# Loads of x three stages later, and two stores a stage later, in a hand-ordered two-layer convolution kernel

## The chip, the cores and the metric

The kernel runs on one core of one Trainium2 chip. The metric is device time in microseconds (us) of one launch; the times shown are those of whole runs, and the profile is of one further execution, taken by the hardware profiler.

## The reference

The input is x, 32 images of 256 channels of 32 x 32 pixels in float32. Two layers follow each other, each added to its own input.

```python
def _gn(v, G=32, eps=1e-5):                # group norm: 32 groups of 8 channels, over all pixels
    ...
    return ((g - m) / jnp.sqrt(s + eps)).reshape(v.shape)

# layer 0: 3x3 convolution, 256 -> 256, with operands and result rounded to a short float format
x = x + _L0_conv_ref(_gn(x), L0_conv_weight, L0_conv_bias)
# layer 1: involution. Each pixel makes its own 7x7 weights, 16 groups of 16 channels
x = x + _L1_conv_ref(_gn(x), L1_conv_w1, ...)
#   y   = relu(bn(w1 @ x))                  256 -> 64 channels
#   w   = w2 @ y + b2                       64 -> 16 groups x 49 taps, for each pixel
#   out = sum over the 49 taps of w[group, tap, pixel] * x[channel, pixel + tap]
```

## The kernel before, in words

An image stays in SBUF as one tile `x_{b}` (128 partitions, 2 halves of the channels, 1024 pixels). The pool `xpool` has five such tiles, so the load of image b can start only when the last store of image b-5 has landed. The same tile is read by the first group norm, gets the convolution added to it, then the involution, and is stored.

The involution is done by TensorE as matrix products over a banded matrix. The path of these bands is what the DMA engines mostly carry:

- `weights(b, r0)` (line 402): TensorE makes the tap weights of four rows (line 410, into PSUM tiles `pw`), VectorE adds the bias and puts them into a ring in SBUF, `w_sb` (line 428).
- `scatter(b, k)` (line 466): seven DMAs of 160 KB, all on SyncE's queue, write the weights of eight rows from `w_sb` to a scratch tensor `wd` in DRAM (line 477). There are four such k for an image.
- `load_bands(b, k)` (line 479): sixteen DMAs of 70.2 KB read `wd` back into one of three `band` buffers (line 490). Fourteen of them are issued by GpSimd, two by SyncE (`SHARE = 8`).
- `sums(b, m)` (line 501): TensorE multiplies a band with the pixels (line 515); the band k serves m = 2k and 2k+1. `add_windows(b, m)` (line 523) lets VectorE add the result to x (line 531).

`front(b)` (line 284) is a generator that does everything of an image ahead of that: the sums and squares of the first group norm (ScalarE, line 219), the normalised image `xq` (line 278), 72 matmuls of the convolution (line 332), VectorE's rounding `q` and addition to x (lines 346, 348), the second group norm, the normalised `xn` (line 278), the 64 matmuls of `py` (line 380), the activation `y` (line 387), and the transposed pixels (lines 395, 399). Its first two steps are ScalarE's sums over the two halves of the freshly loaded x.

The order on every engine is written out by hand. The loop at the end goes over stages n; an image takes 16 stages, and each kind of work has a lag against its image. Work that is due in one stage is issued in the order of the loop's body, and each engine's queue holds it in that order. Several fronts are under way at once, of images up to three ahead, and in each stage the older image's front is issued first. Stages below are counted as n modulo 16, where stage 0 is `sums(b, 0)`:

| stage | on SyncE's queue before the change |
|---|---|
| 1 | load of x for image b+4 (`LOAD = -63`) |
| 3 | scatter k=0 of the next image, then two DMAs of band k=3 |
| 7 | scatter k=1 of the next image, then two DMAs of band k=0 of the next image |
| 8, 9 | (not SyncE: ScalarE's first sums over the x of image b+4, `FRONT = -56`) |
| 11 | scatter k=2 of the next image, two DMAs of its band k=1 |
| 12 | store of the first half of image b |
| 13 | scatter k=3 of the next image |
| 15 | store of the second half of image b, two DMAs of band k=2 of the next image |

`load_x` (line 102) issues two DMAs of 512 KB; `store` (line 533) one of 512 KB. The DMAs of SyncE use eight completion semaphores in turn, and so do those of GpSimd, so a DMA is issued only when the one eight places ahead of it has landed.

Of the kernel before, what the change touches and what calls it, by code (L numbers as in the profile page):

```python
# [14 lines left out]
B, C, H, W = 32, 256, 32, 32  # L15
# [28 lines left out]
M = K * SIDES  # L44
# [19 lines left out]
NPIX = 6  # L64
RING = 24
FRONT = -56
LOAD = -63
LEAD = 18


# [1 line left out]
def tile_quant_conv_then_involution(  # L72
# [29 lines left out]
    def load_x(b):  # L102
        xt = xpool.tile([P, CH, N], F32, tag="x", name=f"x_{b}")
        for h in range(CH):
            nc.sync.dma_start(xt[:, h], x[b, h * P : (h + 1) * P])
        return xt
# [15 lines left out]
    x_tiles = {0: load_x(0)}  # L122
# [75 lines left out]
    def quantize_weights():  # L198

        for kh in range(CH):  # L200
            nc.vector.tensor_scalar(wq[:, kh], staged[kh], F16_MAX, -F16_MAX, ALU.min, ALU.max)
            nc.gpsimd.memset(bands[kh], 0.0)
        nc.gpsimd.memset(w_sb, 0.0)
# [198 lines left out]
    def weights(b, r0):  # L402

        pws = [ps_w.tile([P, 2, 2, SW], F32, tag=f"pw{i}", name=f"pw{i}") for i in range(2)]
        for r in range(2):
            for t in range(T):
                for i in range(2):
                    half = slice(i * CR, (i + 1) * CR)
                    dj = slice(2 * t, min(2 * t + 2, K1))
                    nc.tensor.matmul(  # L410
                        pws[i][t * TW : (t + 1) * TW, r, : dj.stop - dj.start],
                        y_sb[b % 2][half, (r0 // 2 + r) * W : (r0 // 2 + r + 1) * W],
                        w2_sb[half, dj],
                        start=True,
                        stop=True,
                    )
        for i in range(2):
            for e in range(2):
                p = P if e == 0 else (K1 // 2) * TW
                for r, rows, d0, d1, at in ring_pieces(b, r0 + 2 * i):  # L420

                    to = w_sb[:p, e]
                    to = bass.AP(
                        tensor=to.tensor,
                        offset=to.offset + at * WB + K1 - 1 - d0,
                        ap=[to.ap[0], [WB, rows], [WB - 1, d1 - d0], [WIN, G]],
                    )
                    nc.vector.tensor_tensor(  # L428
                        to,
                        pws[i][:p, r : r + rows, e, d0 * G : d1 * G].rearrange("p r (d g) -> p r d g", g=G),  # L430
                        b2_sb[:p, e, d0 * G : d1 * G]
                        .unsqueeze(1)
                        .to_broadcast([p, rows, (d1 - d0) * G])
                        .rearrange("p r (d g) -> p r d g", g=G),
                        ALU.add,
                    )
# [29 lines left out]
    def scatter(b, k):  # L466

        at = (b * H + k * TR) % RING
        for dj in range(K1):
            t, e = divmod(dj, 2)  # L470
            to = bass.AP(
                tensor=wd.tensor,
                offset=wd.offset + k * TR * ROW + dj * WPIX + (K1 - 1 - dj) * WB,
                ap=[[WPIX, TW], [ROW, TR], [1, WB]],
            )
            rows = w_sb[t * TW : (t + 1) * TW, e, at : at + TR]
            nc.sync.dma_start(to, rows.rearrange("p s g r -> p s (g r)"))  # L477

    def load_bands(b, k):

        band = bands[(b * K + k) % NBAND]
        for i in range(JC):
            j = i // 2 + i % 2 * JC // 2
            src = bass.AP(
                tensor=wd.tensor,
                offset=wd.offset + k * TR * ROW + (j + PAD1) * WPIX,
                ap=[[ROW - 1, TR], [JC * WPIX, SIDES], [1, WPIX]],
            )
            queue = nc.sync if i % SHARE == SHARE - 1 else nc.gpsimd
            queue.dma_start(band[j::JC, :, j * WB : j * WB + WPIX], src)  # L490
# [10 lines left out]
    def sums(b, m):  # L501

        k, d = divmod(m, SIDES)
        j0 = 0 if d else PAD1
        band = bands[(b * K + k) % NBAND][:, d]
        px = pixels[(b * K + k) % NPIX][:, d]
        for h in range(CH):
            for v in range(2):
                for g, at, top, f, l in windows(b, m):
                    p = slice(g * KP, (g + 1) * KP)  # L510
                    of = band[p, g * XR + j0 * WB : g * XR + (j0 + WINI) * WB]
                    of = of.rearrange("p (j g r) -> p j g r", g=G, r=WIN)
                    for t in range(T):
                        a = h * T + t
                        nc.tensor.matmul(  # L515
                            at[t * TW : (t + 1) * TW, h, :, f - top : l - top],
                            px[p, a, v * GC : v * GC + TW],
                            of[:, :, 2 * a + v, f - top : l - top],
                            start=(h, v) == (0, 0),
                            stop=(h, v) == (CH - 1, 1),  # L520
                        )

    def add_windows(b, m):

        d = m % SIDES
        to = x_tiles[b].rearrange("p h (r c) -> p h r c", c=W)
        j0 = d * (JC - PAD1)
        for g, at, top, f, l in windows(b, m):
            x_at = to[:, :, f:l, j0 : j0 + WINI]
            of = at.rearrange("p h j r -> p h r j")[:, :, f - top : l - top]  # L530
            nc.vector.tensor_tensor(x_at, of, x_at, ALU.add)  # L531

    def store(b, k):

        cols = slice(k * NT, (k + 1) * NT)
        nc.sync.dma_start(out[b].rearrange("(h p) n -> p h n", p=P)[:, :, cols], x_tiles[b][:, :, cols])
# [3 lines left out]
    per = 2 * M  # L540

    def due(n, lag):

        b, i = divmod(n - lag, per)
        return (b, i) if 0 <= b < B else (None, None)

    with tc.manual_schedule():
        fronts = {}
        for n in range(FRONT, B * per + 2):
            b, i = due(n, FRONT)  # L550
            if i == 0:
                fronts[b] = front(b)
            later = list(fronts)
            for part in range(2):
                for b in list(later):
                    got = next(fronts[b], fronts)
                    if got is fronts:
                        fronts.pop(b)
                    if got is not LATER:
                        later.remove(b)  # L560
            if n == FRONT + CH:
                quantize_weights()
            b, i = due(n, 0)
            if b is not None and i % 2 == 0:
                sums(b, i // 2)
            b, i = due(n, 1)
            if b is not None and i % 2 == 0:
                add_windows(b, i // 2)
                if i // 2 == M - 1:
                    store(b, 1)  # L570
                    x_tiles.pop(b)

            b, i = due(n, 2)
            if b is not None and i == 2 * (M - 1 - SIDES):
                store(b, 0)
            b, i = due(n, -LEAD)
            if b is not None and i % 2 == 0:
                weights(b, i // 2 * WR)

            b, i = due(n, -LEAD + 1)  # L580
            if b is not None and i % 2 == 0:
                for k in range(K):
                    if i // 2 == min((k + 1) * TR // WR, H // WR - 1):
                        scatter(b, k)
            b, i = due(n, LOAD)
            if i == 0 and b > 0:
                x_tiles[b] = load_x(b)

            b, i = due(n, 3 - 4 * NBAND)
            if b is not None and i % 4 == 0:  # L590
                load_bands(b, i // 4)
# [37 lines left out]
```

## Time and profile before

| | |
|---|---|
| time, median of 3 runs | 1401.32 us (1395.67 to 1407.39) |
| the profiled execution's own time | 1399.26 us |
| its span, first to last instruction | 1397.5 us |
| TensorE matmul busy | 1263.0 us, 90% |
| GpSimd busy (DMA descriptors, nearly all) | 1009.8 us, 72% |
| VectorE busy | 926.6 us, 66% |
| ScalarE busy | 727.9 us, 52% |
| bytes moved by DMA | 369.33 MB, mean 264 GB/s |
| mean granted TensorE clock | 0.979 of full speed |

The busy times are sums over one engine's instructions; the issue of a DMA by SyncE is not counted as busy, and is seen in SyncE's own list of waits and in its timeline. The first matmul comes 18 us after the start, the first `add_windows` at 95.6 us, and from there an image takes 41.0 us on average, 2.56 us for a stage. The three loads of x for images 1 to 3 are issued at 21.3, 22.6 and 23.6 us.

### The profile page before, as it was taken

To read this page: it belongs to the slowest core of one execution; us is meant where nothing else is said; L and a number is where in the kernel's file an instruction comes from. 1 tells how busy PE (TensorE), PEld (TensorE's weight loads), DVE (VectorE), ACT (ScalarE), POOL (GpSimd) and SP (SyncE) were. 2 spreads that over 40 slices of the span, in tenths; PEclk is the share of its full clock that TensorE was granted. 3 is DMA by queue.
4 is the path that set the end of the run, shared out by engine and by line. 5 is a ranking of instruction groups with operands and counts; after the bars stand their busy time and mean duration, and the time that the engine had idled before them with its cause. 6 is when DMAs were issued, how large, how long until landed. Compare 5 with 4: busy or idle time off the path is not lost.

```text
span 1397.5 us, 70073 instructions
## 1 busy us (share of the span) xinstructions
PE 1263.0 (90%) x29440; PEld 801.1 (57%) x29440; DVE 926.6 (66%) x3179; ACT 727.9 (52%) x1699; POOL 1009.8 (72%) x1818
## 2 busy tenths in 40 slices
PE   4899999999999999998998999999999999999765
PEld 2455565556656566565655565655555655556544
DVE  3567677666776667676776666776666776777552
ACT  5865556455655546565554556463556564553200
POOL 9067777777777777778777777767776767777785
PEclk9999999999999999999999999999999999999876
DMA  6099999999999999999999999999999999999996
GB/s 215 16 248 276 253 283 289 280 274 272 286 284 274 287 278 281 278 285 274 280 287 272 272 273 282 263 278 275 273 282 267 265 282 277 282 264 269 252 257 187
DMA packets 366232, 369.33 MB, mean 264 GB/s; under 512 B 78624, under 2 KB 308192, under 8 KB 365664
## 3 DMA queue, kind: packets, MB, share of 16 engines
q1 hardware_dynamic: 279904, 235.72, 57.3%
q0 software_dynamic: 86016, 129.14, 34.7%
q8 instruction: 234, 3.83, 1.2%
q14 instruction: 78, 0.64, 0.2%
HBM read 183.81 MB, written 180.74 MB: 261 GB/s over the span
## 4 chain that ended last, share of the span: by engine, by line
PE 49%; DMA 30%; issue 6%; POOL 5%; DVE 4%; SPq 3%; ACT 2%; POOLq 0%; DVEq 0%; ACTq 0%
DMA band<-wd 23%; PE pc L332 20%; PE acc L515 15%; PE pw L410 9%; DMA wd<-w_sb 6%; POOL band L490 5%; PE py L380 3%; SPq L477 3%; DVE w_sb L428 2%; PE pt L395 2%; ACT junk L219 1%; DVE x L531 1%; DMA band<-in_w 1%; DMA x<-in_x 0%; ACT xn L278 0%
## 5 line engine op out<-in xcount | busy, mean ns | idle before, releaser
L490 POOL DMA_DIRECT2D band<-wd x1792 | 977.9, 548 | 375.4 <-DMA band<-wd 239.4
L428 DVE TENSOR_TENSOR w_sb<-pw,b_sb 128x16 f32<-128x16 f32 (+9 forms) x1920 | 454.3, 349 | 374.7 <-PE pw L410 362.0
L332 PE MATMUL pc<-xq,wq 128*128 128x496 f16 (+3 forms) x2304 | 535.1, 378 | 28.1 <-ACT xq L278 21.3
L515 PE MATMUL acc<-band,pixels 64*32 64x190 f32 (+1 forms) x16384 | 419.1, 323 | 73.8 <-DMA band<-wd 32.3
L515 PEld LDWEIGHTS acc<-band,pixels 64*32 64x32 f32 x16384 | 297.5, 108 | 165.9 <-issue 99.1
L332 PEld LDWEIGHTS <-wq 128*128 128x128 f16 x2304 | 206.5, 98 | 323.5 <-issue 110.2
L410 PE MATMUL pw<-w_sb,y 64*32 64x224 f32 (+1 forms) x8192 | 297.8, 333 | 24.1 <-issue 23.1
L531 DVE TENSOR_TENSOR x<-acc,x 128x380 f32<-128x380 f32 (+1 forms) x512 | 261.6, 511 | 35.7 <-PE acc L515 26.8
L410 PEld LDWEIGHTS pw<-w_sb,y 64*32 64x32 f32 x8192 | 183.2, 106 | 58.4 <-issue 40.6
L399 ACT COPY pixels<-pt 128x512 f32<-128x512 f32 x128 | 73.6, 575 | 234.7 <-PE pt L395 234.7
L219 ACT ACTIVATE junk<-x 128x512 f16<-128x512 f32 (+1 forms) x192 | 146.4, 763 | 14.7 <-DVE x L348 7.4
L219 ACT ACTIVATE junk<-x,mean 128x1024 f16<-128x1024 f32 x128 | 147.1, 1149 | 4.3
L250 ACT ACTIVATE s<-back,eps 128x2 f32<-128x2 f32 x64 | 18.9, 296 | 200.3 <-DVE back L235 200.2
L278 ACT ACTIVATE xn<-x,off,rstd 128x512 f32<-128x512 f32 x128 | 96.1, 800 | 0.0
L346 DVE TENSOR_SCALAR q<-pc 128x512 f16<-128x512 f32 x128 | 87.2, 681 | 12.5 <-PE pc L332 12.3
L348 DVE SCALAR_TENSOR_TENSOR x<-q,bias_sb,x 128x512 f32<-128x512 f16 x128 | 92.1, 719 | 0.2
L395 PEld LDWEIGHTS pt<-ident,xn 128*128 128x128 f32 x512 | 63.6, 142 | 27.1 <-issue 2.5
L395 PE MATMUL pt<-ident,xn 128*128 128x128 f32 x512 | 77.8, 275 | 1.2 <-ACT pixels L399 1.2
L278 ACT ACTIVATE xq<-x,off,rstd 128x1024 f16<-128x1024 f32 x64 | 76.0, 1228 | 1.4 <-PE pc L332 1.3
L240 ACT ACTIVATE mean<-back 128x2 f32<-128x2 f32 x64 | 12.7, 198 | 119.2 <-DVE back L235 119.0
L380 PEld LDWEIGHTS py<-xn,w_sb 128*64 128x64 f32 x2048 | 62.7, 138 | 16.3 <-issue 9.1
L380 PE MATMUL py<-xn,w_sb 128*64 128x64 f32 x2048 | 67.5, 224 | 2.3 <-ACT xn L278 1.8
(40 smaller groups left out, 369.5 us busy)
## 6 DMA issues: line engine op xcount, KB each, us to landing
wd<-w_sb SPq DMA_DIRECT2D x896, 160.0 KB
band<-wd POOLq DMA_DIRECT2D x1792, 70.2 KB, 5.0
x<-in_x SPq DMA_DIRECT2D x64, 512.0 KB
out<-x SPq DMA_DIRECT2D x64, 512.0 KB
band<-wd SPq DMA_DIRECT2D x256, 70.2 KB
band<-in_w SPq DMA_DIRECT2D x2, 1152.0 KB
w_sb<-in_w SPq DMA_DIRECT2D x2, 196.0 KB
wd<-band SPq DMA_DIRECT2D x2, 180.0 KB
```

Of the source, the lines that this page charges most:

```text
L219: nc.scalar.activation(junk[:, n0:n1], src[:, h, n0:n1], func, bias=bias, accum_out=self.sums[:, i : i + 1])
L278: nc.scalar.activation(dst, src, AF.Identity, bias=self.off[:, one], scale=self.rstd[:, one])
L332: nc.tensor.matmul(pc.rearrange("p (r c) -> p r c", c=W)[:, r0 - nt * RT : r1 - nt * RT, c0:c1], wq[:, kh, k, mh * P : (mh + 1) * P], xq[: ...
L346: nc.vector.tensor_scalar(q, pc, F16_MAX, -F16_MAX, ALU.min, ALU.max)
L348: nc.vector.scalar_tensor_tensor(xt[:, mh, cols], q, bias_sb[:, mh : mh + 1], xt[:, mh, cols], ALU.add, ALU.add)
L380: nc.tensor.matmul(py[i * CR : (i + 1) * CR, cols], w1_sb[:, kh, :], px[:, r : r + 2], start=kh == 0, stop=kh == CH - 1,)
L395: nc.tensor.transpose(pt[:, i, h * P : (h + 1) * P], xn[:, h, (m + i) * P : (m + i + 1) * P], ident)
L410: nc.tensor.matmul(pws[i][t * TW : (t + 1) * TW, r, : dj.stop - dj.start], y_sb[b % 2][half, (r0 // 2 + r) * W : (r0 // 2 + r + 1) * W], w ...
L428: nc.vector.tensor_tensor(to, pws[i][:p, r : r + rows, e, d0 * G : d1 * G].rearrange("p r (d g) -> p r d g", g=G), b2_sb[:p, e, d0 * G : d ...
L490: queue.dma_start(band[j::JC, :, j * WB : j * WB + WPIX], src)
L515: nc.tensor.matmul(at[t * TW : (t + 1) * TW, h, :, f - top : l - top], px[p, a, v * GC : v * GC + TW], of[:, :, 2 * a + v, f - top : l - top],
L531: nc.vector.tensor_tensor(x_at, of, x_at, ALU.add)
```

## The change

The loads of x move from stage 1 to stage 4, the store of an image's second half from stage 15 to stage 0 of the next round, and the store of its first half from stage 12 to stage 13. The loop runs one stage longer.

```diff
-LOAD = -63
+LOAD = -60
...
-        for n in range(FRONT, B * per + 2):
+        for n in range(FRONT, B * per + 3):
...
             if b is not None and i % 2 == 0:
                 add_windows(b, i // 2)
-                if i // 2 == M - 1:
-                    store(b, 1)
-                    x_tiles.pop(b)
-
-            b, i = due(n, 2)
+
+            b, i = due(n, 3)
             if b is not None and i == 2 * (M - 1 - SIDES):
                 store(b, 0)
+            b, i = due(n, 2)
+            if b is not None and i == 2 * (M - 1):
+                store(b, 1)
+                x_tiles.pop(b)
```

The order of instructions on TensorE, VectorE, ScalarE and GpSimd is the same in both kernels; only SyncE's queue differs. In each round of 16 stages it now reads:

```
before: scatter k=3 | store 2nd half | band k=2 x2 | load x x2 | scatter k=0 x7 | band k=3 x2 | scatter k=1 x7 | ...
after:  scatter k=3 | band k=2 x2 | store 2nd half | scatter k=0 x7 | band k=3 x2 | load x x2 | scatter k=1 x7 | ...
```

The store of the first half stands between the band k=1 and scatter k=3 in both. At the start, the load of image 3 comes after the first scatter instead of before it.

## The prediction

> **What bounds the kernel now.** I read the page first, then the two lists of waits (all engines, and SyncE's queue), then SyncE's timeline and ScalarE's for one round of 16 stages.
>
> ```profile
> PE 1263.0 (90%) x29440; PEld 801.1 (57%) x29440; DVE 926.6 (66%) x3179; ACT 727.9 (52%) x1699; POOL 1009.8 (72%) x1818
> DMA  6099999999999999999999999999999999999996
> ...
> PE 49%; DMA 30%; issue 6%; POOL 5%; DVE 4%; SPq 3%; ACT 2%; POOLq 0%; DVEq 0%; ACTq 0%
> ```
>
> TensorE is busy 90% and the DMA engines 90% or more in nearly every slice; the chain that ended last is half TensorE and a third DMA. So there are two near-bounds, and neither leaves much room.
>
> ```profile
> POOL band L490 <- DMA band<-wd: 239.4, 295, 2.9
> PE acc L515 <- DMA band<-wd: 32.3, 19, 6.5
> POOL band L490 <- PE acc L515: 2.6, 1, 2.6
> PE py L380 <- ACT xn L278: 1.8, 2, 1.3
> ```
>
> GpSimd, which issues 14 of each band's 16 DMAs, waits 239 us for its own DMA eight places back, and almost never for a band buffer to be freed by TensorE (2.6 us): it goes from band to band without a break. Sorted by image (images 3 to 28), TensorE idles 2.5 us of the 41.0 us of an image: 1.57 before `sums`, 0.78 before `weights`, 0.13 before the convolution. Of the 1.57, 0.45 stand before the sums of band k=2, 0.51 before the two groups of k=1, 0.40 at k=0, and 0.21 elsewhere. That is the most a better order could give back. Before `py` TensorE practically never waits; that is the cover the change draws on.
>
> ```profile
> SPq L105 <- DMA out<-x: 85.3, 27, 4.1
> SPq L477 <- DVE w_sb L428: 163.4, 78, 41.5
> ```
>
> SyncE stands 85.3 us in 27 loads of x, 3.2 us in each, until the store of the tile's earlier image has landed. In one round:
>
> ```profile
> 625.36 1.07 SPq L536 DMA_DIRECT2D out<-x  x1
> 626.52 1.60 SPq L490 DMA_DIRECT2D band<-wd  x2
> 631.09 1.13 SPq L105 DMA_DIRECT2D x<-in_x  x2
> 632.57 5.90 SPq L477 DMA_DIRECT2D wd<-w_sb  x7
> 638.57 1.56 SPq L490 DMA_DIRECT2D band<-wd  x2
> 642.11 5.54 SPq L477 DMA_DIRECT2D wd<-w_sb  x7
> ```
>
> The gap from 628.12 to 631.09 is that wait. ScalarE on the same image:
>
> ```profile
> 645.78 1.04 ACT L219 ACTIVATE junk<-x 128x1024 f16<-128x1024 f32 x1
> 646.73 0.19 ACT L219 ACTIVATION_READ_ACCUMULATOR junk<-x 128x1 f32 x1
> 646.82 1.50 ACT L278 ACTIVATE xn<-x,off,rstd 128x512 f32<-128x512 f32 x2
> 648.23 1.04 ACT L219 ACTIVATE junk<-x 128x1024 f16<-128x1024 f32 x1
> 649.18 0.19 ACT L219 ACTIVATION_READ_ACCUMULATOR junk<-x 128x1 f32 x1
> 649.27 1.50 ACT L278 ACTIVATE xn<-x,off,rstd 128x512 f32<-128x512 f32 x2
> 655.06 0.78 ACT L387 ACTIVATE y<-py,bn_shift,bn_scale 128x512 f32<-128x512 f32 x1 [1.03 <-PE py L380]
> ```
>
> The 128x1024 `junk<-x` are the first readers of the load issued at 631.09. Right between and behind them stand the `xn` of an older image, which `py` on TensorE needs next.
>
> [...]the packets of scatter k=0 (640 B each) begin 3.1 us after their issue at 632.57,[...] against 1.2 us for scatter k=1 issued at 642.11. [...]bytes and packets do not change here, so no DMA time is saved by the move itself. [...]In this trace the load of x is issued 0.65 us (median) after the last packet of the store it waits for; I use 0.65.
>
> **The change part by part.**
>
> *The store of the first half* keeps its place in SyncE's queue, between the DMAs of band k=1 and scatter k=3. It already waits for the same VectorE additions. Cost 0.
>
> *The store of the second half* goes behind two band DMAs. These land 10.5 us (median) before TensorE wants that band; the 14 of GpSimd land 2.5 us before and decide. So they gain nothing, and the store's only follower that counts is the load of x, which goes later itself. The store no longer holds these two up while it waits for VectorE (23.0 us in 11 waits, 11.5 of it at the end). Cost 0, at most 0.1 us an image.
>
> *The load of x, what it removes.* The wait of 3.2 us goes: the store has four stages (10 us) to land instead of two. What is next is scatter k=0, and it waits for VectorE's `w_sb`. It is issued 1.27 us (mean) after VectorE's last piece, so it can come 1.3 us earlier, not 3.2. It lands 3.7 us before GpSimd begins the band (the tightest of the four k, but not binding: GpSimd's idle time before that band is 0.35 us on average). Gain: up to 0.2 us an image, below 6 us in all; I count 0.
>
> *The load of x, what it adds.* Times below are medians from the first `add_windows` of the round. Before: issue at 3.9, first packet 1.1 us later, last one 6.6 us after issue, at 11.0 (in some rounds a little earlier). ScalarE's turn for the first half is at 17.8 and for the second half 2.45 us later, so the load had some 7 to 9 us to spare. After: nine instructions of SyncE come before it, seven of the scatter and two of the band, which end at 13.6. With the 1.3 us saved the issue is at 12.3 to 13.7. The queue ahead is not empty: in the old trace the scatter's last packet comes at 16.3 and the band's at 17.2; 1.3 us earlier that is 15.9, and x's own service, last packet to last packet, takes 5 to 6 us (11.0 after a band at 4.9). That gives 21.0, and 21.6 with the semaphore, against ScalarE's turn at 20.2. The load is late by about 1.4 us in the median.
>
> *Who waits for that.* ScalarE is a queue: behind the late `junk<-x` are the two pairs of `xn`. They end 1.72 us (median; 0.7 to 2.9) before `py` starts on TensorE. So the median delay is just hidden, and the late ones are not. Laying "issue at the old end of the band DMAs, plus 7.4 us, plus 0.65" over the recorded ScalarE turns of images 6 to 30 gives a mean delay of 1.8 us and, beyond a cover of 1.72, a mean stall of 0.76 us at `py`; with 6.7 us it is 0.42, with 7.4 and the 1.3 us saved 0.42, with 6.0 it is 0.19. I take 0.76, since the queue ahead is fuller than any row shows. Where TensorE would next have waited for a band (0.40 us at k=0), the stall is partly swallowed; I take off 0.30. Left: 0.46 us x 27 images = 12.4 us. ScalarE itself then has idle time of 1.0 us before `y` and 5.9 before the next variance, so the delay does not pile up. VectorE waits on the same sums (`across`), but has 4.5 us of idle time soon after.
>
> *Scatter k=1* now stands behind x in the ring and lands about 2 us later. It landed 5.2 us before GpSimd's first DMA of that band, so 3 us remain: 0, at worst 0.3 us an image.
>
> *GpSimd's own wait* (9.5 us an image) is where the DMA engines' load shows. x moves off the end of band k=2 and the beginning of k=3 to the end of k=3. k=3 lands 3.6 us before need, k=2 only 2.5, so this can help by up to 0.6 us an image; it can also cost as much, since the hole in DMA traffic is left empty at 4 to 7 us of the round. No row shows it: bounds -17 and +17 us, taken as 0.
>
> *Start.* The load of image 3 goes from 23.6 us to behind the first scatter (66 to 72 us), lands near 80 instead of long before, and ScalarE takes it at 77.4: about 2.5 us late in a stretch where every stage is chained. I count 2.6 us.
>
> *Sum*: 12.4 + 2.6 = +15.0 us on the profiled execution's own 1399.3 us, 1414.3. That execution lay 2.1 us under the median of the runs, so against the median 1401.3 I forecast 1416.
>
> **The rivals.**
>
> *Hidden (1402).* If x is served in 6 us and scatter k=0 comes 1.3 us earlier, the stall at `py` is 0 by the same table. For it: the 7 to 9 us to spare before. Against: the full ring ahead of x.
>
> *Faster (1384).* One mechanism: x leaves the stretch in which GpSimd fetches band k=2, which TensorE waits for most. If the 0.45 us there go, and half of the 0.34 before the first sums of k=0, it is 0.62 x 28 = 17 us. It decides from the point where x lands before ScalarE's turn in nearly all images and GpSimd's wait falls from 9.5 to below 9.0 us an image. Against: GpSimd is served one band after another, and what k=2 gains k=3 loses.
>
> *Much slower (1442).* The cover of 1.72 us is worth nothing because the delayed ScalarE queue also holds VectorE: the whole 1.8 us less 0.3 reaches TensorE, 1.5 x 27 = 41 us.
>
> *The change does not do what it says*: only for the store of the first half, as shown; it moves no time.
>
> **How the numbers follow.** Forecast (1406 to 1430) 0.42, hidden 0.31, faster 0.14, much slower 0.13. About 1% is what a measurement of this kernel can tell from no change, here 1387 to 1415. Of the forecast 0.08 lies under that bound. So faster 0.14, same 0.31 + 0.08 = 0.39, slower 0.34 + 0.13 = 0.47. The range 1386 to 1446 leaves out half of the faster case and a little of the slowest.
>
> **What would show it.** Right: SyncE's wait for `out<-x` before line 105 is near 0; "ACT junk <- DMA x" appears with some 20 to 50 us in 15 or more waits; "PE py <- ACT xn" grows from 1.8 us to over 10. Wrong: no ScalarE wait for x (then hidden or faster), or a loss that appears at the sums instead, with GpSimd's wait for its own DMAs well over 239 us, which would mean that the DMA traffic's order decides and not the lateness of x.

## The result, and the profile after

The changed kernel takes 1410.88 us (median of 12 runs) against 1394.44 us for the kernel before in the same session; the ratio on record is 1.0092, 95% interval 1.0066 to 1.0119 (that of the two medians is 1.0118). A second measurement, beside three of the experiments, gave 1.0058 (1.0026 to 1.0091). The profiled execution took 1411.24 us, 12.0 us more than the one before. The size is what was forecast; the way it comes about is not.

The page of the changed kernel, its totals, granted clock, DMA share and chain:

```profile
span 1409.5 us, 70074 instructions
PE 1264.7 (90%) x29440; PEld 805.6 (57%) x29440; DVE 925.7 (66%) x3179; ACT 730.1 (52%) x1699; POOL 1009.7 (72%) x1818
...
PEclk9999999999999999999999999999999999999986
DMA  5099999999899999999999999999999999999995
...
PE 53%; DMA 24%; DVE 6%; issue 6%; ACT 4%; SPq 3%; POOL 3%; POOLq 0%; DVEq 0%; ACTq 0%
```

Every engine does the same work in nearly the same busy time. DMA gives up six points of the chain; TensorE takes four, VectorE and ScalarE two each. So a little more of this one chain runs through ScalarE's queue, as expected, but most of it does not. Some waits, the first line from the kernel before, the others from the changed one:

```profile
DVE across L229 <- ACT junk L219: 19.3, 15, 7.0
...
DVE across L229 <- ACT junk L219: 60.3, 27, 7.0
PE acc L515 <- DMA band<-wd: 38.5, 24, 4.8
ACT junk L219 <- DMA x<-in_x: 36.3, 26, 3.0
PEld py L380 <- ACT xn L278: 10.8, 13, 2.2
PE py L380 <- ACT xn L278: 7.9, 9, 2.1
```

ScalarE waits for x in 26 images, 36.3 us. `py` waits 7.9 us where it waited 1.8. SyncE's wait for the store in front of line 105, 85.3 us before, is no longer in its list. In its place SyncE waits longer for VectorE's weights in front of the scatters:

```profile
SPq L477 <- DVE w_sb L428: 246.6, 102, 43.7
```

That is 83 us more than the 163.4 before. One round of SyncE's queue:

```profile
600.13 0.40 SPq L536 DMA_DIRECT2D out<-x  x1
602.01 5.74 SPq L477 DMA_DIRECT2D wd<-w_sb  x7
607.85 1.87 SPq L490 DMA_DIRECT2D band<-wd  x2
609.82 1.19 SPq L105 DMA_DIRECT2D x<-in_x  x2
611.47 6.54 SPq L477 DMA_DIRECT2D wd<-w_sb  x7
```

SyncE goes from the store to scatter k=0 with no hold for a store (it stands 1.48 us in between); the load of x follows the band, with scatter k=1 on its heels. In ScalarE's timeline of the same image:

```profile
617.71 1.06 ACT L219 ACTIVATE junk<-x 128x1024 f16<-128x1024 f32 x1 [2.71 <-DMA x<-in_x]
618.68 0.19 ACT L219 ACTIVATION_READ_ACCUMULATOR junk<-x 128x1 f32 x1
618.77 1.50 ACT L278 ACTIVATE xn<-x,off,rstd 128x512 f32<-128x512 f32 x2
```

The number in brackets is idle time: ScalarE stood 2.71 us before it could start on x. So the predicted lateness is real. Whether it costs anything is the question of the first experiment.

### The profile page after: what moved, and what is told of

The parts are those of the page before. It is cut to its first block, busy times and chain, and to the rows that moved or that the text cites. A ratio compares the mean times of both kernels' runs of the same rounds, so it can differ in the third digit from the quotient of the medians.

```text
span 1409.5 us, 70074 instructions
## 1 busy us (share of the span) xinstructions
PE 1264.7 (90%) x29440; PEld 805.6 (57%) x29440; DVE 925.7 (66%) x3179; ACT 730.1 (52%) x1699; POOL 1009.7 (72%) x1818
## 4 chain that ended last, share of the span: by engine, by line
PE 53%; DMA 24%; DVE 6%; issue 6%; ACT 4%; SPq 3%; POOL 3%; POOLq 0%; DVEq 0%; ACTq 0%
PE pc L332 21%; PE acc L515 17%; DMA band<-wd 15%; PE pw L410 10%; DMA wd<-w_sb 5%; DVE w_sb L428 4%; DMA x<-in_x 4%; POOL band L490 3%; SPq L477 3%; PE py L380 3%; PE pt L395 2%; ACT junk L219 2%; ACT xn L278 1%; DMA band<-in_w 1%; DVE x L531 1%
## 5 line engine op out<-in xcount | busy, mean ns | idle before, releaser
L515 PE MATMUL acc<-band,pixels 64*32 64x190 f32 (+1 forms) x16384 | 417.6, 324 | 78.2 <-DMA band<-wd 38.5
L410 PE MATMUL pw<-w_sb,y 64*32 64x224 f32 (+1 forms) x8192 | 293.2, 335 | 25.6 <-issue 25.4
L219 ACT ACTIVATE junk<-x 128x512 f16<-128x512 f32 (+1 forms) x192 | 146.9, 765 | 54.8 <-DMA x<-in_x 36.3
L250 ACT ACTIVATE s<-back,eps 128x2 f32<-128x2 f32 x64 | 18.9, 296 | 193.8 <-DVE back L235 193.8
L240 ACT ACTIVATE mean<-back 128x2 f32<-128x2 f32 x64 | 12.6, 197 | 119.9 <-DVE back L235 119.9
```

The source lines that it names most:

```text
L219: nc.scalar.activation(junk[:, n0:n1], src[:, h, n0:n1], func, bias=bias, accum_out=self.sums[:, i : i + 1])
L410: nc.tensor.matmul(pws[i][t * TW : (t + 1) * TW, r, : dj.stop - dj.start], y_sb[b % 2][half, (r0 // 2 + r) * W : (r0 // 2 + r + 1) * W], w ...
L515: nc.tensor.matmul(at[t * TW : (t + 1) * TW, h, :, f - top : l - top], px[p, a, v * GC : v * GC + TW], of[:, :, 2 * a + v, f - top : l - top],
```

## The experiments

Every ratio below is against the kernel before on the same chip. The runs were made in three groups of four kernels; the first and the third group ran on the same chip, the second on another.

**1. Take ScalarE's wait away, leave the DMAs.** The first sums read a constant tile instead of x, in every image but the first; each still takes 1.04 us (median), and every DMA stays. The kernel leaves out the true sums. Theory A is that of the prediction: the late x holds ScalarE, and through it `py` and VectorE. The rival B: the order of the DMA traffic slows what TensorE needs.

```diff
+    still = wq[:, :, :4].rearrange("p h k c -> p h (k c)")
...
-            gn.add_up(xt, 0, h, 0, N, AF.Identity)
+            gn.add_up(still if b else xt, 0, h, 0, N, AF.Identity)
```

> The changed kernel, except that ScalarE's first two sums of each image but the first read a constant tile instead of the freshly loaded x (their values are left out, their duration stays). All DMAs stay where the change put them. Theory A (the late x holds ScalarE, and through it `py` and VectorE): the loss goes, ratio to the kernel before 0.998 to 1.003, ScalarE's wait for x near 0, VectorE's wait `across` back from 60 us to about 20. Rival B (the order of the DMA traffic slows the bands): the loss stays, 1.007 to 1.012.

> The same edit of the two sums in the kernel before, as a control: x is long there when ScalarE reads it, so both theories expect 0.998 to 1.002. If this is itself faster or slower, the run of the changed kernel with the edit is read against it.

Measured: the changed kernel with the edit 1.0107 (1.0075 to 1.0138), the kernel before with it 1.0004 (0.9984 to 1.0024). In the waits of the changed kernel with the edit, ScalarE's wait for x is gone and VectorE's is nearly back where it was; the third line is from the kernel before with the edit:

```profile
PE acc L517 <- DMA band<-wd: 59.8, 33, 6.4
DVE across L229 <- ACT junk L219: 24.1, 24, 7.2
...
PE acc L517 <- DMA band<-wd: 45.2, 23, 6.0
```

The cause that the prediction named is removed, and the loss stays in full. Theory A falls: the lateness at ScalarE is a symptom that carries no part of the loss that can be seen. The wait for bands is longer than in the kernel before with the same edit, 59.8 against 45.2 us, as it is without the edit (38.5 against 32.3).

**2. One part of the change at a time.** Load alone: `LOAD = -60` in the kernel before. Stores alone: the changed kernel with `LOAD = -63`.

> Only the load of x moves (LOAD = -60); both stores stay where they were. Theory A expects the whole loss, 1.007 to 1.012, with 30 to 40 us of ScalarE's wait for x. If the stores share in the loss, less than 1.006.

> Only the stores move (LOAD stays -63). The second half's store now stands directly in front of the load of x that waits for another image's same store in SyncE's queue, so SyncE is held longer in front of scatter k=0: 4 to 6 us an image instead of 3.2. Theory A: x still lands in time, the scatter comes 1 to 3 us later but has 3.7 us to spare, so 0.999 to 1.006. Rival B: the store out of the way of band k=2 helps, 0.993 to 0.999.

Measured: load alone 1.0211 (1.0175 to 1.0247), stores alone 1.0001 (0.9982 to 1.0020). The load alone costs more than the whole change. The stores alone cost nothing, though SyncE's hold in front of the load grows:

```profile
SPq L105 <- DMA out<-x: 137.2, 27, 5.7
```

That is 5.1 us an image instead of 3.2, for no time at all. The load alone was run again in the third group (the text says another chip; it came to be the same one):

> The load of x moved and both stores where they were, once more, on another chip. If its 1.021 was of that chip: 1.006 to 1.012, like the whole change. If the store in front of band k=2 really costs a further per cent together with the late load: 1.017 to 1.024.

Measured: 1.0152 (1.0118 to 1.0186). That touches the first interval, and the load alone stays above the whole change; in the first group itself it was 1.0211 against 1.0107 for the changed kernel without ScalarE's wait. With the late load, the move of the stores is worth something: 1.0058 and 1.0092 for the whole change against 1.0152 and 1.0211 without it, 0.6 to 1.5% between any two, in different groups. Why is not settled. The profiles show where it lies: TensorE's idle time with no wait that the profile shows ("issue", see the next experiment) is 2.29 us an image in both runs of the load alone, against 1.62 in the kernel before and 1.59 in both profiles of the whole change.

**3. Where TensorE stands idle.** I sorted TensorE's idle time (gaps over 0.15 us, images 3 to 28) by its place in the round. It is 2.48 us an image before and 2.83 after. In the kernel before, 0.85 of it lies at 12 to 20 us of the round; after, 0.47. At 20 to 24 us it is 0.16 before and 0.99 after. The load of x moved in the same direction: its packets come at 5 to 11 us before, at 12.6 to 19.6 after. One such gap in the changed kernel's TensorE timeline:

```profile
568.58 1.52 PE L515 MATMUL acc<-band,pixels 64*32 64x190 f32 x64
574.35 1.37 PE L410 MATMUL pw<-w_sb,y 64*32 64x224 f32 x32 [4.25 <-issue]
575.66 3.44 PE L332 MATMUL pc<-xq,wq 128*128 128x512 f16 x9
579.02 1.52 PE L515 MATMUL acc<-band,pixels 64*32 64x190 f32 x64
580.34 0.96 PE L410 MATMUL pw<-w_sb,y 64*32 64x224 f32 x32
581.22 1.04 PE L332 MATMUL pc<-xq,wq 128*128 128x496 f16 x4
```

Two things are in it. First, the gap of 4.25 us ends on "issue", that is, nothing the profile shows was being waited for. In others of these gaps TensorE stops in the middle of one group of `weights`, between two matmuls that wait for no one:

```profile
323.95 0.73 PE L410 MATMUL pw<-w_sb,y 64*32 64x224 f32 x17
326.18 0.60 PE L410 MATMUL pw<-w_sb,y 64*32 64x224 f32 x15 [1.50 <-issue]
```

17 of the 32 are done, then 1.50 us of nothing, then 15. What does go with these gaps is a DMA that no line of the kernel issues. The page lists the queues:

```profile
q8 instruction: 234, 3.83, 1.2%
```

234 packets, each of 16384 B: the instruction packets. 71% of TensorE's idle time before (1.77 of 2.48 us an image) and 64% after (1.82 of 2.83) ends between 0.9 and 1.75 us after the end of such a packet; in 55 of the 78 gaps before, it is 1.25 to 1.75 us. With the same gaps shifted in time at random, the share is 15%. Idle time that ends so is called idle time behind an instruction packet below, and a fetch wait in the recorded expectations. That TensorE stands there for want of its own instructions is my reading of the queue's name and of this nearness in time; no run shows it. The gaps that end behind such a packet are in any case the largest part of TensorE's idle time. The packets themselves take as long as ever (1.06 us before, 1.04 after, median); if anything is late, it is before the packet starts, and that the trace does not show.

The totals also say what the place alone hides. The idle time behind such a packet moved from 12 to 20 us of the round (0.52 us an image before, none after) to 20 to 24 us (0.14 before, 0.93 after), and grew in all by only 0.05 us, in the repeated profile by 0.20. What grew more evenly is TensorE's idle time that ends on a band: 0.47 us an image before and 0.81 in both profiles of the change; with the edit of experiment 1, 0.69 and 1.04.

Second, the nine matmuls after the gap take 3.44 us instead of the 2.08 that nine of them take elsewhere (the last row shows the first four of nine). The granted clock was at half from 575.0 to 578.4 us. Between 40 us and image 29 the profile of before has 2 windows of half clock, 6.8 us in sum; that of the changed kernel 10, 41.0 us; of the run without ScalarE's wait 10, of the load alone 11 and 10. Each of these 12 windows of the profiles before and after is 3.4 or 6.8 us long, and within a profile they begin at multiples of 3.41 us from one another. In the 3.41 us right before each of the 12, TensorE idled between 1.83 and 3.27 us. Cut at the same multiples, the same part of the two profiles (40 us to image 29) gives 710 other stretches of 3.41 us at full clock, with no window right behind them, and in none of them did it idle more than 1.94 us. Not every measurement of the change shows more windows: the repeated profile of the changed kernel has 4 and still 1.0058, and the kernel before with the edit of experiment 1 has 4 at 1.0004.

**4. Is it the size of the pieces of x?** Theory C: the burst of large packets of x is what makes the gaps behind instruction packets long. In the first pair the load is cut into four DMAs, in the last one it is issued from ScalarE's queue, past the scatter.

```diff
-            nc.sync.dma_start(xt[:, h], x[b, h * P : (h + 1) * P])
+            for c in range(2):
+                cols = slice(c * N // 2, (c + 1) * N // 2)
+                nc.sync.dma_start(xt[:, h, cols], x[b, h * P : (h + 1) * P, cols])
```

> The changed kernel as it is, on the same chip as the three runs beside it. 1.007 to 1.012, with about 10 windows of half the TensorE clock between 40 us and the 29th image.

> The changed kernel with each load of x cut into four DMAs of 256 KB (2048 B to a packet) instead of two of 512 KB (4096 B). Theory C[...]:[...] the idle time of TensorE at 20 to 24 us of the round falls from 0.9 to below 0.6 us an image, and the ratio to 1.000 to 1.005. Rival B (order and amount of the traffic alone): no difference to the changed kernel, 1.007 to 1.012.

> The same cut in the kernel before. Theory C: a little faster, 0.993 to 0.999, since there too some 0.5 us an image of fetch waits stand behind the load of x (12 to 20 us of the round). Rival B: 0.998 to 1.002.

> The changed kernel with the loads of x issued from ScalarE's queue, at the same stage, instead of SyncE's, so that they stand behind no scatter and no band. Lateness of x: gone, ScalarE has it some 3 us earlier, at the price of two DMA issues an image on ScalarE[...]. Theory C:[...] 1.000 to 1.006. Rival B: 1.007 to 1.012.

Measured: the changed kernel 1.0058 (1.0026 to 1.0091); with x in four pieces 1.0056 (1.0032 to 1.0080); the kernel before with x in four pieces 1.0053 (1.0032 to 1.0073); the load from ScalarE's queue 1.0107 (1.0076 to 1.0137). The pieces change nothing after the change: the idle time of TensorE behind an instruction packet at 20 to 24 us stays 0.99 us an image (0.93 in the changed kernel). Before the change they cost half a per cent instead of gaining; four DMAs also take four places in SyncE's queue instead of two, and the two effects were not separated. The load from ScalarE's queue is early enough, and its stall is another one: 1.40 us an image before the first sums of band k=2, 0.33 in the repeated changed kernel. Theory C, that the size of x's packets does it, falls for packets of half the size; smaller ones were not tried.

**5. Take the bytes away, leave the order.** Theory D: what costs is the transfer itself where it now stands. Rival E: the order of the queue and its waits. From image 5 on, only the last 64 of the 1024 columns are loaded, into five fixed tiles; they overlap the store of the second half, so the hold in the kernel before stays. The kernel leaves out the other columns, and what remains of an earlier image stands in them.

```diff
-        xt = xpool.tile([P, CH, N], F32, tag="x", name=f"x_{b}")
+        xt = x_five[b % 5]
+        cols = slice(0 if b < 5 else N - N // 16, N)
         for h in range(CH):
-            nc.sync.dma_start(xt[:, h], x[b, h * P : (h + 1) * P])
+            nc.sync.dma_start(xt[:, h, cols], x[b, h * P : (h + 1) * P, cols])
```

> The kernel before, with the loads of x of images 5 to 31 cut to their last 64 of 1024 columns (64 KB instead of 1 MB an image; the rest of the tile stays as an earlier image left it, so the outputs are others). Number and order of DMAs, waits and the hold for the store stay. Both theories: faster than before by up to the 1 MB's share of the DMA time, 0.97 to 1.00. It is the reference for the next run.

> The same cut in the changed kernel. Theory D (the loss is the transfer of x itself, at the place where it now stands: its megabyte delays what TensorE needs next[...]): without the megabyte the two kernels differ by less than 0.3%, and the fetch waits at 20 to 24 us of the round fall from 0.9 to below 0.4 us an image. Rival E (the order of SyncE's queue and its waits, whatever is moved): this one stays 0.6 to 1.0% slower than the kernel before with the same cut.

Measured: the kernel before with thin loads 0.9656 (0.9629 to 0.9683), the changed kernel with thin loads 0.9523 (0.9487 to 0.9558). Neither theory said that: without the bytes the changed order is *faster*, 1338.93 against 1357.82 us, 18.9 us or 1.4%. The waits of the thin kernel before still have the hold, and the thin changed kernel has none of it:

```profile
SPq L108 <- DMA out<-x: 90.9, 27, 4.5
```

TensorE's idle time behind an instruction packet at 20 to 24 us is 0.01 us an image in the one and 0.05 in the other. So the order that the change makes is a good one once the bytes are away: TensorE's idle time falls from 1.55 to 1.16 us an image, that which ends on a band from 0.62 to 0.27. Which part of the order does it is not shown. The hold goes and scatter k=0 starts earlier (3.8 instead of 6.5 us into the round), but both are so in the load alone too (3.8 us), which loses. And the megabyte costs much more in its new place. In the old one it is worth 3.4% (1.0000 against 0.9656). In the new one it is worth 5.4 to 5.7% (1.0058 or 1.0092 against 0.9523).

The trace's DMA packets say why that can be. Averaged over images 4 to 27, the DMA engines' busy share in the two microseconds that begin at the time named (overlaps count, so it can pass 1) is:

```
us of the round            4      6      8     10     12     14     16     18     20
before, all             0.88   0.93   1.03   1.08   1.08   0.96   0.97   0.97   0.98
before, thin x, all     0.80   0.72   0.85   0.95   0.97   0.95   0.95   0.92   0.98
changed, all            0.85   0.97   0.98   0.98   0.91   1.00   1.04   1.10   1.11
changed, thin x, all    0.91   0.98   0.97   1.00   0.87   0.89   0.95   0.97   0.98
```

In the old place x fills a hole: SyncE is held, no scatter is under way, and without x the engines would be at 0.72 to 0.85. In the new place scatter k=0 has already filled that hole, and x falls in front of scatter k=1, into a stretch that is then over-full (1.04 to 1.11 at 16 to 22 us), just where TensorE's idle time of 20 to 24 us begins. But the kernel before has an over-full stretch too, 1.03 to 1.08 at 8 to 14 us, so the share alone does not say why one costs more than the other.

That bytes and place together do it is shown by the four kernels. Through what they reach TensorE is not shown by a run of its own. In the profiles the bytes add about as much idle time behind an instruction packet in either place (0.88 us an image before, 1.03 in the changed kernel), but idle time that ends on a band only in the new one (0.27 to 0.81, against 0.62 to 0.47 in the old one). So the bands are the nearer suspect.

**6. Half here, half there.** The load of the first half of the channels at stage 1, the second at stage 4, the stores as before.

```diff
-                x_tiles[b] = load_x(b)
+                x_tiles[b] = load_x(b, halves=[0])
+            b, i = due(n, LOAD + 3)
+            if i == 0 and b > 0:
+                load_x(b, x_tiles[b], [1])
```

> The kernel before, with the load of the first half of the channels at its old stage 1 and that of the second half at the new stage 4; stores as before. Theory D: two bursts of half a megabyte let the queue recover in between, the fetch waits of both places shrink: 0.994 to 1.001. Rival E: half of the loss of the moved load, 1.003 to 1.010.

Measured: 1.0038 (1.0020 to 1.0057), with 0.45 us an image of idle time behind an instruction packet at 20 to 24 us, half of the changed kernel's. It lies about halfway, as E said; half a megabyte is in the worse place, and the first half still waits for the store (83.7 us in 27 loads). The parts of experiment 5 do not simply add up here: half of what the new place costs more would be 1.0 to 1.1%, with no gain from the order, and 0.38% is measured. No kernel here with all of x loaded beats the one before.

## Why the prediction was right, and where it was not

- *SyncE's hold goes, the store of the first half keeps its place.* Right; the wait of 85.3 us is gone. Scatter k=0 starts 2.1 us earlier (5.9 to 3.8 us into the round, median), more than the 1.3 counted. Whether that alone is worth the 0 that was put on it is open; all moves in the queue together are worth 1.4% once x is out of the way (18.9 us).
- *x comes late to ScalarE.* Right. Issue 11.1 us into the round (forecast 12.3 to 13.7), last packet at 19.6 (forecast 21.0), ScalarE waits in 26 images. The forecast put x behind what SyncE issued before it; the changed kernel's trace shows that for scatter k=0: x's first packet begins at 12.6, and 2% of its packets (median) begin before the scatter's last one at 13.1.
- *The lateness costs 12.4 us through `py`.* This is the step that failed. Without ScalarE's wait the changed kernel is still at 1.0107, so the lateness carries no part of the loss that can be seen. The idle time before `py` rose to only 0.12 us an image (0.20 in the repeated profile), against 0.46 counted. The cover held better than the laid-over table said; that what did pass was swallowed by other waits is likely and not shown.
- *"No row shows it: bounds -17 and +17 us, taken as 0"*, for the order of the traffic. This was the mis-sized term. Read from the thin kernels it consists of two: about -19 us for the order, and +27 to +32 us that the megabyte costs more in its new place than in its old one (18.9 plus a loss of 0.58 to 0.92% of 1400 us). This takes the order to be worth the same with the bytes and without, which no run shows. Each of the two lies beyond its bound; only the net, 8 to 13 us, lies within. The forecast of 15 us came out by luck: a wrong term had nearly the right size.
- *What x would hit.* The prediction looked for band k=3, with its 3.6 us to spare. In the new place TensorE's idle time grew before the sums of m=5 (0.03 us an image before, 0.48 after, behind an instruction packet) and before `py`, while other gaps behind such packets shrank; what grew in total is the idle time before all sums, 1.58 to 1.91 us an image, and in it the part that ends on a band, 0.47 to 0.81.
- *The signs.* Of the three for "right", two came (SyncE's wait near 0; 36.3 us for x in 26 waits). The third, "over 10" us before `py`, did not: 7.9, in the repeated profile 6.1. That was the one that stood for the cost. Of the sign for "wrong", the first half came, a loss at the sums (1.58 to 1.91 us an image). The second half, GpSimd's wait well over 239 us, did not:

```profile
POOL band L490 <- DMA band<-wd: 251.5, 311, 4.1
```

In the repeated profile that wait was 234.2 us, below the one before. TensorE's own idle time by place and by what ended it would have been the better sign.
- *The stores of the second half: 0.* Right with the early load (1.0001), wrong with the late one (0.6 to 1.5% between the kernels with the stores moved and without).
- *Start: 2.6 us.* The first `add_windows` comes at 96.8 us instead of 95.6; 1.2 us.

## What to carry to other kernels

Where DMA engines are nearly full, as here (busy 90% or more in 37 of the 40 slices of the page before), price a moved transfer by the traffic at its two places and not by its slack alone: the same megabyte cost 3.4% in a hole of the traffic and 5.4 to 5.7% 7 to 8 us later, in front of the next burst. A consumer that is seen to wait after a change is a suspect, not a cause; take its wait away with the DMAs left in place before it is named. And when TensorE stops inside a group of matmuls that wait for nothing, look at the instruction queue's packets; but compare the totals before and after: here such gaps moved and hardly grew, 1.77 and 1.82 us an image.

## What the runs showed that I had not expected

- TensorE's largest idle share in a kernel of 29440 matmuls, unrolled, goes with the packets of the instruction queue: 1.77 us an image of 2.48 ends 0.9 to 1.75 us after one of these 16384 B packets. With the thin loads the 1.77 is 0.89 in the kernel before, and the 1.82 is 0.79 in the changed one.
- The two windows of half clock in the profile of before come right after stretches of 3.41 us with 2.23 and 2.70 us of idle time, each one stall. A stall of 2.63 us at 712.1 us has no window behind it; cut at the same multiples of 3.41 us, it falls into two stretches, with 0.82 and 1.81 us.
- Loading x by four DMAs of 2048 B packets instead of two of 4096 B costs the kernel before 0.5% (1.0053, 1.0032 to 1.0073) and the changed one nothing.
- SyncE may be held 137.2 us in all instead of 85.3 at no cost in time (1.0001).
